# One kernel for six sublayers: ScalarE's order written out in two stages, weights quantized in pieces, transposes of a pair ahead of their copies

## The chip, the core and the metric

The kernel runs on one NeuronCore of a Trainium2 chip. A core has engines with queues of their own: TensorE (PE, matrix products and transposes, into PSUM), VectorE (DVE), ScalarE (ACT), GpSimd (POOL) and SyncE (SP, which here only starts transfers). They meet at semaphores. An engine works through its own queue in order. The metric is the device time of one execution in microseconds, lower is better; the median of several runs stands for a kernel. One more execution was profiled, and what the profile says is of that one.

## What is computed

The input `x` is 8 sequences of 1024 tokens with 256 numbers each, 8192 tokens in float32. Six sublayers follow, each on a layer norm of `x` and added to `x`:

```python
x = x + 0.5 * _L0_ffn_ref(_layernorm(x), w_gate, w_up, w_down)        # fp4
x = x + _L0_attn_ref(_layernorm(x), Wqkv_w, Wqkv_b, out_w, out_b, gamma_raw)   # decay
x = x + 0.5 * _L0_ffn_ref(_layernorm(x), w_gate, w_up, w_down)        # fp4 again
x = x + 0.5 * _L1_ffn_ref(_layernorm(x), W1, b1, W2, b2)              # ternary
x = x + _L1_attn_ref(_layernorm(x), w_q, w_k, w_v, w_o, gate, memories, memory_norms)
x = x + 0.5 * _L1_ffn_ref(_layernorm(x), W1, b1, W2, b2)              # ternary again
```

The fp4 feed-forward quantizes every operand in blocks of 16 numbers: a scale (largest magnitude / 6), rounding to the grid 0, 0.5, 1, 1.5, 2, 3, 4, 6, and the scale again. It computes `silu(x Wg) * (x Wu)`, quantizes that too, and multiplies by `Wd` (704 hidden numbers). The weights are quantized inside the kernel. The ternary feed-forward divides each weight matrix by its mean magnitude, rounds to -1, 0 or 1, and uses a GELU between (1024 hidden numbers).

The decay attention is a linear attention with one decay `sigmoid(gamma_raw)` per head. The memory attention, 16 heads of 16, is this:

```python
sq = elu1(q); sk = elu1(k)                     # elu + 1
out_m = einsum('bhsd,mhde->mbhse', sq, memories) / clip(einsum('bhsd,mhd->mbhs', sq, memory_norms))
weights = softmax(mean over s of the divisors)
mem_out = sum over m of weights * out_m
num = einsum(sq, cumsum(sk x v));  den = einsum(sq, cumsum(sk))
out = sigmoid(gate) * mem_out + (1 - sigmoid(gate)) * num / den,  then  out @ w_o.T
```

## The kernel before

All of `x` stays in SBUF, 16 tiles `X[g]` of 4 x 128 tokens. A group is 512 tokens, a unit 128 of them: 16 groups, 64 units. The six stages run one after the other, called at the end of `macaron_kernel`: `ffn_fp4(True, "decay")`, `attn_decay("fp4")`, `ffn_fp4(False, "ternary")`, `ffn_ternary(False, "memory")`, `attn_memory("ternary")`, `ffn_ternary(True)`. Only the first prepares weights beside its units (`prepare`).

**Order.** An instruction given to `pin` (lines 172 to 188) follows the last pinned one of its engine: the order is written by hand. What is not pinned is placed by the framework's scheduler, which may draw it forward to where its inputs are ready. Before the change TensorE and VectorE are pinned nearly everywhere; ScalarE is pinned nowhere in the fp4 stages and the memory attention. `behind` (line 190) makes a block of preparation start behind the last pinned instructions.

**Statistics.** `statistics(sizes, dues)` (line 232) splits the layer norm's statistics of all groups into small shares for VectorE (`bn_stats`, `bn_aggr`, then a seed and four Newton steps), handed out by `advance(u)` one unit at a time. `PLANS` says how many groups are taken together and when they are due. The first set of a stage is computed by `begin` during the last units of the stage before. `normalize` (line 273) is two ScalarE instructions for each of a group's four tiles.

**The start** (lines 388 to 461). The raw weights and the first tile come in by DMA on the queues of SP, ScalarE and GpSimd. `scale_part` and `round_part` quantize the halves of the gate and up weights and the first `xn`: maxima and rounding on VectorE, magnitudes (`Abs` with a factor) on ScalarE, both multiplications on GpSimd; TensorE turns the weights.

**An fp4 stage** (`ffn_fp4`, line 602). For unit `i` of group `g` (`j` = `i` mod 4), `hidden(i)` makes for two halves `q` the products `pg` and `pu` (line 685), `sg = silu(pg)` on ScalarE (694) and `h = sg * pu` on VectorE (695). `scale` (632) and `round_` (650) quantize `h`; `q_sc` is a small ScalarE copy, `qp` holds magnitudes. `turn(i-2)` transposes `h` into two PSUM tiles `pt` which ScalarE copies to `ht`; `down(i-3)` multiplies by `wd` into `po` (727), and VectorE adds it to `x` (736). The next group's `xn` is normalized at `j` = 0, scaled at 1, rounded at 2; at `j` = 3, between `pg` and `pu` of the second half, `norm_turn` transposes it (`transpose_group`, line 350): four transposes, a copy (361), four transposes, a copy. The pool of `pt` has two buffers, shared by `xt` and `ht`.

Beside the units of the first stage (`first`, line 741): at 0 and 1 `prep_down`, at 1 the turning of the down weights and `load_a0`, at 5 `prep_decay` (the decays' exponentials and tables), at 6 and 9 the loads of `w1`, `w2`, at 8 and 11 `prep_ternary` in one piece (sum on VectorE, total `pa` by a matmul in the bank of `po`, two halves rounded on VectorE), at 12 `prep_memory`.

**The memory attention** (`attn_memory`, line 1202) is a pipeline: in step `i` the keys and values of unit `i`, the scores of unit `a` = `i-1`, the weighted sum of `b` = `i-2`, the division of `c` = `i-3`, and outputs of `d`, `e`. `keys(i)` (1369) makes the products `pkv` and three ScalarE results: `vz` (1387), `kd` (1394, not in the last unit of a sequence) and `qz` (1398), two masked copies of the queries `sq`, which need nothing of `keys` itself. The scores `sc` (917) of the next step need `qz`. TensorE's order in a step: memory products `pmo` (1410) among scores `sc`, `py`, `psd`, in the last step of a group the divisors `pr`, then the transposes `pyt` of `y` and `pn` of `nt` (in that last step of a group both in one PSUM tile, `pyn`), a projection `pk` or `pq` of a group two ahead (1015), the output `po`, and `keys(i)`. VectorE makes `at` (926), `mo` (1423), `rw` (1549), `y`, and the sum into `x` (1619). ScalarE further makes `nt`, `state`, `yt`, `ee` (1255) and `xt`. Groups 0 to 2 are projected in an opening before the steps; units 56 to 63 have no projection left to do.

Of the kernel before, what the change touches and what calls it, by code (L numbers as in the profile page):

```python
# [17 lines left out]
P = 128  # L18
# [20 lines left out]
def macaron_kernel(  # L39
# [52 lines left out]
    w_f0 = f0_stack.enter_context(tc.tile_pool(name="w_f0", bufs=1))  # L92
    raw_stack = ExitStack()
# [34 lines left out]
    gsig = w_l1.tile([P, H], F32, name="gsig")  # L128
    nc.sync.dma_start(out=gsig, in_=gate.partition_broadcast(P))
# [102 lines left out]
    def statistics(sizes, dues):  # L232
# [40 lines left out]
        def normalize(dst, g, only=None):  # L273
            for j in range(G) if only is None else (only,):
                n = G * g + j
                nc.scalar.activation(
                    dst[:, j, :], X[g][:, j, :], AF.Identity, bias=lb[:, n : n + 1]
                )
                nc.scalar.activation(dst[:, j, :], dst[:, j, :], AF.Copy, scale=lr[:, n : n + 1])
# [16 lines left out]
            (GB + 1, 2, 3, 4, NG), [max(0, G * (g - GB) - 3) for g in range(NG)]  # L296
# [95 lines left out]
    with (  # L392
# [6 lines left out]

        def scale_part(v, bank, at):  # L400
# [15 lines left out]
            def round_part():  # L416
                mg = prep_q.tile([P, nb * 16], F32, tag="q_mg", name="q_mg")[:np_]
# [30 lines left out]
        round_g()  # L448
        weights_turn(wg_n, wg, 0)
        round_u()  # L450
# [3 lines left out]
        round_x()  # L454
# [7 lines left out]

    def prep_down(c):
        fp4_round(wd_n[:, c, :], fp4_scale(wd_n[:, c, :], raw, nc.vector, pin), raw, nc.gpsimd, pin)
# [11 lines left out]
    a0_stack = ExitStack()  # L476
    A0 = SimpleNamespace()

    def load_a0():
        w_a0 = a0_stack.enter_context(tc.tile_pool(name="w_a0", bufs=1, side="right"))  # L480
# [6 lines left out]
        A0.lng = w_a0.tile([P, H + 2], F32, name="lng")  # L487
        A0.dec = w_a0.tile([P, 4, 4, P], F32, name="dec")
        A0.gq = w_a0.tile([P, 2, P], F32, name="gq")
        A0.gk = w_a0.tile([P, H], F32, name="gk")  # L490
        A0.gs = w_a0.tile([P, 2], F32, name="gs")
# [5 lines left out]
        nc.sync.dma_start(out=A0.lng[:, 0:H], in_=gamma.partition_broadcast(P))  # L497
        nc.sync.dma_start(out=A0.lng[:, H : H + 2], in_=gamma_rep.rearrange("(m p) -> p m", p=P))

    def prep_decay(prep):  # L500
# [4 lines left out]

        ea = prep.tile([P, H + 2], F32, tag="ea", name="ea")
        nc.scalar.activation(ea, A0.lng, AF.Abs)
# [94 lines left out]
    def ffn_fp4(prepare, after):  # L602
        with ExitStack() as st:
# [94 lines left out]
            def rounding(i):  # L698

                parts = []  # L700
                if i % G == 2 and i // G + 1 < NG:
                    parts.append(x_part(i // G + 1))
# [980 lines left out]
```

## Time and profile before

| | us |
|---|---|
| median of 3 runs (2856.53 to 2856.86) | 2856.61 |
| profiled execution | 2854.04 |
| its span, first to last instruction | 2851.3 |

The stages, from the profile's windows (busy us of each engine; edges read from the timeline to some us):

| stage | window, us | length | PE | DVE | ACT | POOL |
|---|---|---|---|---|---|---|
| start | 0 to 45 | 45 | 9.8 | 34.5 | 16.5 | 24.2 |
| fp4, first | 45 to 650 | 605 | 540.2 | 464.1 | 270.4 | 251.1 |
| decay attention | 650 to 1115 | 465 | 459.1 | 304.7 | 187.1 | 4.5 |
| fp4, second | 1115 to 1675 | 560 | 528.6 | 429.8 | 246.9 | 235.0 |
| ternary, first | 1675 to 1940 | 265 | 262.3 | 181.4 | 166.5 | 0.2 |
| memory attention | 1940 to 2584 | 644 | 582.5 | 498.7 | 317.8 | 299.1 |
| ternary, second | 2584 to 2851 | 267 | 262.4 | 176.1 | 162.5 | 0.0 |

How to read it: where an engine's busy time is near the length of its window, that engine sets the stage's time. Lines of the profile give, for a group of instructions, its source line, engine, operation, output and inputs by name, and the idle time in front of it with what released it: `PE pt L712 <- ACT xt L361` is TensorE waiting, at its instruction of line 712, for ScalarE's instruction of line 361. A busy TensorE is not one at its peak.

Unit lengths, by the starts of `po` at line 727: 7.98 us in a plain unit, 9.05 in a `j` = 3 unit without a wait for `xt`, 10.84 with one. In the memory attention, twelve groups (2038.28 to 2491.70, by `pyn`) take 453.4 us, 37.8 each.

### The profile page before, as it was taken

The page shows a single profiled execution, that of the slowest core. Times are in us where ns is not written, and L with a number is a line of the kernel's source. Part 1 is how long each engine was busy: PE and PEld are TensorE (multiplying, and loading weights), DVE is VectorE, ACT ScalarE, POOL GpSimd, SP SyncE. Part 2 cuts the span into 40 slices and gives each one's busy share as a digit, 9 for nine tenths or more (in the row PEclk, how much of TensorE's full clock was granted, in tenths as well). Part 3 has the DMA queues.
Part 4 walks back from the last instruction along what each step waited for, and adds up shares of the span by engine and source line. Part 5 has one row for each costly group of instructions (what it writes and reads, how often), then busy time and mean ns, then how long its engine had stood idle before and what let it go on. Part 6 is the DMA issues. An engine that isn't in the chain of part 4 may idle for free.

```text
span 2851.3 us, 53491 instructions
## 1 busy us (share of the span) xinstructions
PE 2644.8 (93%) x21536; PEld 1996.1 (70%) x21536; DVE 2089.3 (73%) x4732; ACT 1367.7 (48%) x3000; POOL 814.1 (29%) x760
## 2 busy tenths in 40 slices
PE   3779999999999998999999999998999999988999
PEld 2557777776676666677776779995666666667998
DVE  7787878776666667887878778555788877877654
ACT  3534444444434333444444456565455555435665
POOL 4434444430000002444444410001455455531000
PEclk9889999999999999999999999999999999999999
DMA  5100000000000000000000000000000000000011
GB/s 166 32 17 1 1 1 1 1 1 1 2 2 2 2 2 1 1 1 1 1 1 1 1 1 1 1 1 1 2 2 2 2 2 2 2 2 16 30 38 38
DMA packets 26228, 27.04 MB, mean 9 GB/s; under 512 B 5116, under 2 KB 25084, under 8 KB 25980
## 3 DMA queue, kind: packets, MB, share of 16 engines
q1 hardware_dynamic: 24838, 21.66, 2.4%
q8 instruction: 169, 2.77, 0.4%
q10 hardware_dynamic: 998, 1.44, 0.2%
q14 instruction: 79, 0.65, 0.1%
q0 software_dynamic: 144, 0.52, 0.1%
HBM read 15.23 MB, written 8.39 MB: 8 GB/s over the span
## 4 chain that ended last, share of the span: by engine, by line
PE 72%; DVE 16%; POOL 4%; ACT 4%; issue 2%; DMA 0%; POOLq 0%; DVEq 0%; ACTq 0%
PE po L874 9%; PE po L727 8%; PE ph L848 8%; PE pg L685 7%; PE pu L685 7%; PE py L1001 4%; PE sc L917 4%; PE po L1015 4%; PE pk L1015 4%; PE pkv L1015 3%; PE pq L1015 3%; DVE h L656 3%; PE py L983 2%; DVE qp L636 2%; DVE xn L656 1%
## 5 line engine op out<-in xcount | busy, mean ns | idle before, releaser
L727 PE MATMUL po<-wd,ht 128*128 128x256 f32 (+1 forms) x1536 | 359.9, 384 | 7.0 <-DVE x L736 6.5
L685 PE MATMUL pu<-wu,xt 128*128 128x352 f32 x1024 | 348.9, 463 | 11.0 <-DVE h L695 10.8
L685 PE MATMUL pg<-wg,xt 128*128 128x352 f32 x1024 | 348.5, 462 | 6.5 <-ACT sg L694 6.0
L727 PEld LDWEIGHTS po<-wd,ht 128*128 128x128 f32 (+1 forms) x1536 | 285.7, 193 | 45.1 <-DVE x L736 8.3
L660 POOL TENSOR_TENSOR h<-h,q_sc 128x704 f32<-128x704 f32 x128 | 177.5, 1387 | 451.9 <-DVE h L656 451.9
L685 PEld LDWEIGHTS pu<-wu,xt 128*128 128x128 f32 x1024 | 193.3, 192 | 114.5 <-DVE h L695 11.9
L695 DVE TENSOR_TENSOR h<-sg,pu 128x352 f32<-128x352 f32 x256 | 129.7, 516 | 187.4 <-PE pu L685 179.8
L685 PEld LDWEIGHTS pg<-wg,xt 128*128 128x128 f32 x1024 | 194.6, 191 | 100.2 <-ACT sg L694 10.9
L874 PE MATMUL po<-w,hl 128*128 128x256 f32 x1024 | 250.5, 282 | 1.1 <-DVE hl L859 1.1
L874 PE MATMUL po<-w,hh 128*128 128x256 f32 x1024 | 249.8, 282 | 0.0
L1582 POOL TENSOR_TENSOR y<-y,mo 128x256 f32<-128x256 f32 x256 | 210.2, 821 | 131.6 <-DVE y L1575 117.9
L656 DVE SCALAR_TENSOR_TENSOR h<-qp,h 128x704 f32<-128x704 f32 x256 | 227.2, 888 | 18.4 <-ACT qp L653 13.9
L859 DVE TENSOR_TENSOR hl<-hf,hh 128x512 fp32r<-128x512 f32 x256 | 168.0, 686 | 64.7 <-ACT hh L857 60.4
L848 PE MATMUL ph<-xh,w 128*128 128x512 f32 x512 | 203.6, 399 | 0.9 <-DVE x L1619 0.5
L694 ACT ACTIVATE sg<-pg 128x352 f32<-128x352 f32 x256 | 118.2, 462 | 177.7 <-PE pg L685 177.7
L848 PE MATMUL ph<-xl,w 128*128 128x512 f32 x512 | 200.6, 393 | 0.0
L644 POOL TENSOR_TENSOR h<-h,q_rs 128x704 f32<-128x704 f32 x128 | 177.6, 1387 | 71.4 <-DVE q_rs L640 54.2
L874 PEld LDWEIGHTS po<-w,hl 128*128 128x128 f32 x1024 | 195.0, 190 | 2.4 <-DVE hl L859 1.7
L874 PEld LDWEIGHTS po<-w,hh 128*128 128x128 f32 x1024 | 194.3, 190 | 1.8
L926 DVE TENSOR_TENSOR at<-sc,tri 128x512 f32<-128x512 f32 x256 | 171.4, 670 | 20.3 <-PE py L1001 17.2
L856 ACT ACTIVATE hf<-ph,b1c 128x512 f32<-128x512 f32 x256 | 167.7, 701 | 17.5 <-PE ph L848 17.4
L926 DVE TENSOR_TENSOR at<-sc,dec 128x512 f32<-128x512 f32 x256 | 158.5, 681 | 18.9 <-PE sc L917 18.9
(257 smaller groups left out, 5576.6 us busy)
## 6 DMA issues: line engine op xcount, KB each, us to landing
x<-in_x SPq DMA_DIRECT2D x15, 512.0 KB, 8.9
out<-x SPq DMA_DIRECT2D x15, 512.0 KB, 2.9
raw_w<-in_w_t SPq DMA_DIRECT2D x2, 1024.0 KB
wqkv<-in_wqkv_t SPq DMA_DIRECT2D x1, 768.0 KB
wu_n<-in_w_up ACTq DMA_DIRECT2D x2, 352.0 KB
wg_n<-in_w_gate SPq DMA_DIRECT2D x2, 352.0 KB
wd_n<-in_w_down ACTq DMA_DIRECT2D x1, 704.0 KB, 14.4
x<-in_x POOLq DMA_DIRECT2D x1, 512.0 KB, 10.9
```

The source lines that it names most:

```text
L644: nc.gpsimd.tensor_tensor(vb, vb, rs[:, :, None].to_broadcast([P, nb, 16]), ALU.mult)
L656: nc.vector.scalar_tensor_tensor(v, mg, FP4_LEAST, v, ALU.max, op)
L660: nc.gpsimd.tensor_tensor(vb, vb, sc[:, :, None].to_broadcast(list(vb.shape)), ALU.mult)
L685: nc.tensor.matmul(ps, lhsT=xt[:, k, j * P : (j + 1) * P], rhs=w[:, k, cols], start=(k == 0), stop=(k == 1),)
L727: nc.tensor.matmul(po, lhsT=ht[:kn, c, :], rhs=wd[:kn, c, :], start=(c == 0), stop=(c == len(DCH) - 1),)
L848: nc.tensor.matmul(ph, lhsT=w1[:, k, f * P : (f + 1) * P], rhs=xt[:, k, :], start=(k == 0 and xt is xh), stop=(k == 1 and xt is xl),)
L856: nc.scalar.activation(hf, ph, AF.Gelu, bias=b1c[:, f : f + 1])
L859: nc.vector.tensor_tensor(hl[:, f, :], hf, hh[:, f, :].bitcast(F32), ALU.subtract)
L874: nc.tensor.matmul(po, lhsT=ht[:, f, j * P : (j + 1) * P], rhs=w2[:, f, :], start=False, stop=(f == NF - 1 and ht is hl),)
L926: nc.vector.tensor_tensor(at, sc.rearrange("p m (e t) -> p (m e) t", e=2), weight, ALU.mult)
L1015: nc.tensor.matmul(dst, lhsT=lhsT, rhs=rhs, start=n == 0, stop=n == len(parts) - 1)
L1582: nc.gpsimd.tensor_tensor(yv, yv, mo_c[:, :, :, m, :].rearrange("p r c n -> p c r n"), ALU.add)
```

## The change

- `gamma` and `gate` are loaded at the start, on ScalarE's queue ahead of `wu_n` and `wd_n`; the decays' pool is opened there. The Sigmoid of `gsig`, `ea`, the index tables and the exponentials `dec`, `gq`, `gk`, `gs` move from `prep_decay` and `prep_memory` into the start phase, pinned; `prep_decay` keeps the multiplications by `tri`.
- The start's magnitudes of three operands go to a PSUM tile `mg0`.
- `prep_down` is split: scaling (multiplication now on GpSimd) at units 0 and 1, rounding at 1 and 2, turning at 2.
- `prep_ternary` returns four pinned pieces, run one a unit at 8 to 11 (`w1`, loaded at 6) and 15 to 18 (`w2`, loaded at 13); `prep_memory` moves from 12 to 20.
- In the fp4 stages ScalarE is pinned: `sg`, the `q_sc` copies, the magnitudes, the second `sg`, `xt`, the normalization, `ht`. At `j` = 3 both halves of `xn` are transposed first (`turn_products`); the two copies stand behind the second `sg`.
- In the memory attention ScalarE is pinned in the order of the program. At each step both transposes `pyt` and `pn` come ahead of the copy `yt`. In the last eight units `keys` goes to bank 2 and comes ahead of the output product. `advance` moves behind the sum into `x`. The memory plan takes five groups first instead of three.

The core of the diff:

```diff
+    A0.lng = w_a0.tile([P, H + 2], F32, name="lng")
+    nc.scalar.dma_start(out=A0.lng[:, 0:H], in_=gamma.partition_broadcast(P))
+    nc.scalar.dma_start(out=A0.lng[:, H : H + 2], in_=gamma_rep.rearrange("(m p) -> p m", p=P))
+    gsig = w_l1.tile([P, H], F32, name="gsig")
+    nc.scalar.dma_start(out=gsig, in_=gate.partition_broadcast(P))
...
-            (GB + 1, 2, 3, 4, NG), [max(0, G * (g - GB) - 3) for g in range(NG)]
+            (GB + 3, 3, 4, NG), [max(0, G * (g - GB) - 3) for g in range(NG)]
...
+        mg0 = prep_pq.tile([P, 1024], F32, name="mg0")
...
+        pin(nc.scalar.activation(gsig, gsig, AF.Sigmoid))
...
+        def decays():
...
+            for h in range(H):
+                pin(
+                    nc.scalar.activation(
+                        A0.dec[:, h % HT // 2, h // HT * 2 + h % 2, :], df, AF.Exp,
+                        scale=A0.lng[:, h : h + 1],
+                    )
+                )
...
         ln.normalize(xn, 0)
         begun["fp4"] = (ln, xn)
-        round_g()
+        decays()
+        round_g(mg0)
...
+    def prep_down_scale(c):
+        wd_sc[c] = fp4_scale(wd_n[:, c, :], raw, nc.gpsimd, pin)
+
     def prep_down(c):
-        fp4_round(wd_n[:, c, :], fp4_scale(wd_n[:, c, :], raw, nc.vector, pin), raw, nc.gpsimd, pin)
+        fp4_round(wd_n[:, c, :], wd_sc.pop(c), raw, nc.gpsimd, pin)
...
+        return sums, total, lambda: rounded(0), lambda: rounded(1)
...
+            def prepared(i):
+
+                if 1 <= i < 3:
+                    prep_down(i - 1)
+                if i < 2:
+                    prep_down_scale(i)
+                if i == 2:
+                    prep_down_turn(ps_t, "pt")
...
+                for k, i0 in enumerate((6, 13)):
...
+                    if i0 + 2 <= i < i0 + 6:
+                        raw_w[1][i - i0 - 2]()
...
+            for i in range(NT + 3):
                 g, j = divmod(i, G)
+                ahead = g + 1 < NG
+                h = hp.tile([P, NI], F32, tag="h", name="h") if i < NT else None
                 if i == 0:
-                    norm_turn(0)
-                if i < NG * G:
-                    hidden(i)
+                    xts[0], copied = turn_products(xts[0])
+                    copied()
+                for q in range(2):
+                    if i < NT:
+                        pg = ps_h.tile([P, NHALF], F32, tag="pg", name="pg", bufs=1)
+                        pu = ps_h.tile([P, NHALF], F32, tag="pu", name="pu")
+                        products(i, q, wg, pg)
+                        if q == 1 and j == 3 and ahead:
+
+                            xts[g + 1], copied = turn_products(xts[g + 1][0])
+                        products(i, q, wu, pu)
+                        gated(h, q, pg, pu)
+                    if q == 0:
+                        while copies:
+                            copies.pop(0)()
+                    elif i < NT and j == 3 and ahead:
+                        copied()
+
+                    if 0 < i <= NT and q == (1 if j == 3 else 0):
+                        magnitudes(hs[i - 1][0], qp[:, 0:NI])
...
+                if i < NT and j == 0 and ahead:
+                    norm(g + 1)
+                if 0 <= i - 2 < NT:
+                    turn(i - 2)
...
+                if 0 <= i - 3 < NT:
+                    down(i - 3)
                 if prepare:
...
+                    prepared(i)
...
-            def keys(i):
+            def keys(i, at):
...
-                pkv = bank(3, [P, 2, D], "pkv")
+                pkv = bank(at, [P, 2, D], "pkv")
...
-                nc.scalar.copy(
-                    vz[:, :, 0::2, :],
-                    pkv[:, 1, :].rearrange("p (r e i) -> p r e i", e=2, i=HD),
+                pin(
+                    nc.scalar.copy(
+                        vz[:, :, 0::2, :],
+                        pkv[:, 1, :].rearrange("p (r e i) -> p r e i", e=2, i=HD),
+                    )
                 )
...
-                    nc.scalar.copy(kd, pkv[:, 0, :])
+                    pin(nc.scalar.copy(kd, pkv[:, 0, :]))
...
                 for e in range(2):
-                    nc.scalar.activation(
-                        qz[:, :, e, :], sq[:, :, cols], AF.Copy, scale=pm[:, e : e + 1]
+                    pin(
+                        nc.scalar.activation(
+                            qz[:, :, e, :], sq[:, :, cols], AF.Copy, scale=pm[:, e : e + 1]
+                        )
                     )
...
-                    yt = cp.tile([P, 2, P], F32, tag="yt", name="yt")
-                    nc.scalar.copy(yt, pyt)
-                    ys[d] = yt
                 if 0 <= c < n:
                     nt, mo_c, rw_c = chunk.pop(c)
                     for m in range(2):
                         pin(nc.tensor.transpose(pn[:, m, :], nt[:, m, :], ident))
+                if 0 <= d < n:
+                    yt = cp.tile([P, 2, P], F32, tag="yt", name="yt")
+                    pin(nc.scalar.copy(yt, pyt))
+                    ys[d] = yt
...
-                if 0 <= e < n:
+                def output():
...
+                if elu and 0 <= e < n:
+                    po = output()
...
                 if i < n:
-                    keys(i)
+                    keys(i, 3 if elu else 2)
                 if elu:
                     elu()
+                elif 0 <= e < n:
+                    po = output()
```

## The prediction

> **What bounds the kernel now.** I read the page's busy times and its chain first, then the waits of TensorE stage by stage, then timelines of ScalarE and TensorE around the waits that the change touches.
>
> The busy times and the chain:
>
> ```profile
> PE 2644.8 (93%) x21536; PEld 1996.1 (70%) x21536; DVE 2089.3 (73%) x4732; ACT 1367.7 (48%) x3000; POOL 814.1 (29%) x760
> PE 72%; DVE 16%; POOL 4%; ACT 4%; issue 2%; DMA 0%; POOLq 0%; DVEq 0%; ACTq 0%
> ```
>
> TensorE is busy 2644.8 of 2851.3 us. No arithmetic leaves it, so the change can only work on the 206 us in which it idles. ScalarE, whose order is rewritten, is busy 48%: it can cost only where TensorE waits for one result of it. So I list TensorE's waits: the first fp4 stage, steady part (200 to 640 us), its beginning (45 to 200), and the memory attention (1990 to 2580). Columns: total us, times, longest.
>
> ```profile
> PE pt L712 <- ACT xt L361: 16.5, 10, 1.8
> ```
> ```profile
> PE pa L550 <- DVE t_ab L546: 17.8, 2, 10.4
> PE ptd L470 <- POOL wd_n L348: 9.1, 1, 9.1
> PE pg L685 <- ACT sg L694: 5.2, 3, 4.4
> ```
> ```profile
> PE pyn L1572 <- ACT yt L1567: 12.7, 13, 1.0
> PE py L983 <- DVE mo L1423: 11.2, 16, 1.5
> PE sc L917 <- DVE at L926: 6.7, 7, 1.7
> PE po L1015 <- DVE rw L1549: 4.8, 8, 0.7
> PE pmo L1410 <- DVE lg L1328: 4.6, 4, 3.1
> ```
>
> In the steady fp4 stage one wait is nearly everything; 1120 to 1670, the second fp4 stage, has the same line with 19.6 us in 12, so 36.1 together. In the memory attention the waits are many and small. What is *not* there matters most: no score waits for its queries `qz`. Around 2199 us (TensorE) and 2207 us (ScalarE):
>
> ```profile
> 2198.83 0.38 PE L1015 MATMUL pkv<-wkv,xt 128*128 128x256 f32 x1
> 2199.16 0.50 PE L917 MATMUL sc<-qz,sk 32*128 32x256 f32 x3
> ```
> ```profile
> 2200.75 0.91 ACT L1398 ACTIVATE qz<-sq,pm 128x256 f32<-128x256 f32 x2 [1.13 <-PE pmo L1410]
> 2207.60 0.37 ACT L1387 COPY vz<-pkv 128x256 f32<-128x256 f32 x1 [1.20 <-PE pkv L1015]
> 2207.87 0.38 ACT L1394 COPY kd<-pkv 128x256 f32<-128x256 f32 x1
> ```
>
> The scores start as the key and value products end (2199.16 against 2198.83 + 0.38). The two `qz` writes run at another time, after scores have released a buffer: ScalarE makes them one or two units early.
>
> **The change part by part.** The sums are made in the profiled execution's time, 2854.04 us with a span of 2851.3; the median of the runs, 2856.61, is 2.6 above it, which I add at the end.
>
> *fp4 stages.* A group's four transposes of `xn` go twice into the two PSUM buffers, and TensorE's next transposes (of `h`) wait there for the second copy on ScalarE:
>
> ```profile
> 394.36 0.63 PE L712 MATMUL pt<-ident,h 128*128 128x128 f32 x4 [1.79 <-ACT xt L361]
> ```
>
> In the change both halves are transposed first and ScalarE copies them right behind the second `sg`, under the matmuls of `pu` (4 x 0.38 us). The 36.1 us go. What is late next: a `down` of 2.76 us (twelve matmuls at 395.04) needs the VectorE addition of the one before. When a statistics tile (0.57 us) stands ahead of that addition, I expect about half of it as a wait once a group: 30 x 0.29 = 8.6. The eight normalisation instructions (eight at 0.5 = 4.0 us) now stand in one piece on ScalarE ahead of the `ht` copies; these have a unit's time (7.98 us between two `down`s) until their `down`, which hides the 4.0; uncovered they would cost up to 1 us a group. Sum: -36.1 + 8.6 = **-28**, bounds -36 (no new wait) and -6 (1 us in each of 30 groups).
>
> *The first units.* Between the third and the eleventh `down` (104.92 and 203.95) pass 99.0 us; eight units at the steady pace of 33.0 a group take 66, so 33 go to preparing weights. On ScalarE in that stretch:
>
> ```profile
> 104.33 1.28 ACT L508 ACT_TABLE_LOAD   x1
> 115.39 4.76 ACT L519 ACTIVATE dec<-df,lng 128x128 f32<-128x128 f32 x16
> 120.95 1.28 ACT L694 ACT_TABLE_LOAD   x1
> 122.24 0.47 ACT L694 ACTIVATE sg<-pg 128x352 f32<-128x352 f32 x1
> ```
>
> `sg` at 122.24 stands behind a table, 16 `dec`, three small ones and another table; TensorE waits 4.4 us and its next `pg` takes 2.72 instead of 1.35, `pu` 2.47. Moving these ahead of the units saves 4.4 + 1.4 + 1.1, about 7. The ternary weights are now summed in one unit, totalled in the next and rounded in two more. The total's matmul `pa` writes the bank of `po`; its 17.8 us of waits shrink to the wait for an addition of `x` and the total behind it, by a walk over the VectorE rows 5 and 3: saves 10. Against it: each rounding piece is 1.2 + 2 x 0.7 = 2.6 us on VectorE inside a unit; I charge half, four times, 5; and 16 multiplies of `dec` by `tri` (7.2 us on GpSimd) still run in one go before the scaling of `h`, 2. Sum: -7 - 10 + 5 + 2 = **-10**, bounds -20 (no charge, `pa` quick) and +5 (the roundings and the multiplies in full).
>
> How TensorE runs after a wait matters for all of this: after 4.4 us of idleness `pg` took double, after the 1.79 us above the transposes took 0.63, as the others do; so I charge the waits of 1.5 us below with themselves alone.
>
> On the table loads a rule and the rows differ. The rows show 1.28 us for a load and the activation 0.01 to 0.02 behind it, so four loads fewer are 5.1 us of ScalarE. The Trainium skill, "ScalarE: Activation LUTs", section What ACT_TABLE_LOAD costs, counts a drain of 1.38 us with each switch, some 2.66 in all: by it four loads are 10.6 us, and the first units' sum would be nearer -15 than -10. The rows decide.
>
> *The start.* ScalarE's queue gets three more DMA issues ahead of `wd_n`'s (about 0.47 each) and 16 + 4 exponentials (4.76 + 1.2). TensorE is there busy 18.3 of 55 us, so most hides behind the loads and GpSimd's scaling. The down weights' scaling moves from VectorE to GpSimd, and TensorE already waits 9.1 us for their last GpSimd step: no gain there. **+1**, bounds -3 and +6 (all exponentials in the way).
>
> *Memory attention: what is added.* With ScalarE written out, the order in a unit is `vz`, `kd`, then the two `qz` of the same unit, and the scores that need them are TensorE's next work. On ScalarE: start 0.04 behind the products, 0.27 until `kd` can start, 0.27 until `qz`, 0.91: 1.5 us. Bounds: 1.7 with no overlap (0.04 + 0.37 + 0.38 + 0.91), 1.25 if the first memory products run meanwhile. TensorE's in-order work behind it is the whole unit. Units 1 to 55 pay: 55 x 1.5 = +82, less 2 for seven units without `kd`. In the last eight units, keys now come before the output product (1.03), which leaves 0.5: +4.
>
> *What is removed.* `pyn` behind `yt`: -12.7, since both transposes now precede the copy. The last units' wait for `rw`: -4.8, as the output product moves back. The opening: TensorE stands 5.4 us at 1973.7 behind statistics and the next products take 3.78 for 1.88 and 1.64 for 1.03; the new plan does five groups of statistics in the ternary stage, where VectorE has room: -7.9, less 2.5 for normalisation now behind an exponential. A VectorE that is late catches up in 1.5 us a unit: `at` and `lg` go (-11.3), of `mo` half (-5.6). Sum: 80 + 4 - 12.7 - 4.8 - 5.4 - 16.9 = **+44**. Bounds: at 1.25 with all of `mo` gone, 69 + 4 - 12.7 - 4.8 - 7.9 - 22.5 = +25, or +15 if VectorE's lateness hides in durations too; at 1.7 with nothing caught up, 92 + 4 - 12.7 - 4.8 - 5.4 = +73.
>
> *Total.* -28 - 10 + 1 + 44 = **+7**: 2861 profiled, **2864** as a median. Two nearly equal sums oppose each other, so the sign is weakly held.
>
> **The rivals.**
>
> *The wait is swallowed and the kernel is faster.* In the memory attention VectorE was what ended last in many units (`mo`, `at`, `lg`, 22.5 us of shown waits, more inside score durations: the scores of 2216.67 took 1.87). If 0.7 us of the wait only replaces these in each unit, 55 x 0.7 = 38 are caught up instead of 16.9, and memory costs +22; with fp4 at -34, the first units at -16 and the start at 0 the sum is -28: 2829. It decides from about 0.7 us of VectorE's lateness in a unit. For it: VectorE has 467 of 590 us of work there. Against: in 1990 to 2580 TensorE's whole idleness was 51 us, and 82 cannot fit into it.
>
> *The normalisation block takes the fp4 gain.* Eight instructions of ScalarE in one piece hold up `ht` and the next `sg`. At 1 us a group the fp4 stages give only -6; with the rest as above the sum is +29: 2886. It decides once ScalarE's backlog at the end of the first unit of a group is over the 4 us that lie between the block and the next unit's first `sg`. For it: 4.4 us behind `dec` reached TensorE at once. Against: there ScalarE was held 8.3 us, not 4.
>
> *The scores do not wait.* If `qz` is ready anyway, memory keeps only what is removed (-12.7 - 4.8 - 5.4), -23, and the sum is -60: 2797. Little speaks for it: `qz` of a unit stands behind its `kd` in ScalarE's order, and nothing else writes it.
>
> **How the numbers follow.** 0.2% is 5.7 us, about what can be told from no change. Forecast 0.46 (0.40 of it slower by more, 0.06 within); normalisation block 0.14, slower; swallowed wait 0.34 (0.32 faster, 0.02 within); no wait 0.06, faster. So slower 0.54, same 0.08, faster 0.38. The forecast's own range is 2850 to 2885. For 8 in 10 the range runs from 2815, the faster rival with some 14 us of the bounds, to 2900, the slower one with as much; outside lie no wait (0.06) and the corners where several bounds meet.
>
> **What would show it.** Right: `PE pt <- ACT xt` gone in both fp4 stages and their groups at 33 to 33.6 us; a new line `PE sc <- ACT qz` with 55 waits of about 1.5; memory groups from 37.8 to about 41 us; `pyn <- yt` gone; eight table loads instead of twelve. Wrong: the new line under 0.8 us each (first rival), a line `pg <- ACT sg` or `po <- ACT ht` in the fp4 stages (second), or scores that still follow the products at once (third). A change in the decay attention or the ternary stages of over 3 us would be something that I have not seen.

## The result and the profile after

| | before | after |
|---|---|---|
| median, us | 2856.74 (4 runs, 2856.53 to 2858.43) | 2873.47 (4 runs, 2872.49 to 2878.55) |
| ratio | 1 | 1.0061, 95% interval 1.0043 to 1.0078 |
| profiled execution | 2854.04 | 2872.56 |
| its span | 2851.3 | 2870.9 |

The change makes the kernel slower by 0.6%, by 16.7 us between medians and 19.6 us between spans. Behind this small sum stand large terms of both signs. I compared the starts of the same TensorE instructions in both profiled executions; a stretch that became shorter is negative:

| stretch | before, us | after, us | difference |
|---|---|---|---|
| to the first `down` | 89.0 | 102.9 | +14.0 |
| from there to `down` of unit 20 | 201.4 | 194.1 | -7.3 |
| units 20 to 62, first fp4 stage | 354.5 | 339.0 | -15.5 |
| end of fp4 and decay attention, to the next fp4 stage's first `down` | 493.6 | 492.1 | -1.5 |
| units 0 to 62, second fp4 stage | 528.4 | 508.7 | -19.7 |
| from there to the last `ph` of the first ternary stage | 255.8 | 256.3 | +0.5 |
| from there to the first `ph` of the second ternary stage: memory attention | 661.8 | 709.2 | +47.4 |
| rest | 263.7 | 265.5 | +1.8 |

The page of the changed kernel, busy times and chain:

```profile
PE 2671.9 (93%) x21536; PEld 2018.8 (70%) x21536; DVE 2087.3 (73%) x4715; ACT 1369.2 (48%) x2996; POOL 816.1 (28%) x762
PE 78%; DVE 10%; ACT 6%; POOL 3%; issue 2%; DMA 0%; ACTq 0%; POOLq 0%; DVEq 0%
```

No engine has more instructions to do, and ScalarE's busy time hardly moves (1367.7 to 1369.2). TensorE's rises by 27.1 us for the same 21536 instructions, 22 of them in the memory attention; below, part of a wait is seen to be filled there and so to count as busy. In the chain of work that ended last, VectorE's share fell from 16% to 10% and ScalarE's rose from 4% to 6%. TensorE's waits after the change, in the steady part of the first fp4 stage:

```profile
PE pt L744 <- POOL h L692: 3.3, 2, 2.6
PE pa L589 <- DVE x L768: 2.7, 1, 2.7
```

`pt <- xt`, 16.5 us before, is gone. In its beginning (45 to 200 us):

```profile
PE ptd L539 <- POOL wd_n L360: 10.6, 2, 7.8
PE pg L721 <- ACT sg L732: 9.1, 2, 7.0
PE pa L589 <- DVE x L768: 5.1, 1, 5.1
```

`pa` fell from 17.8 to 5.1 in this window (another 2.7 comes later), but `pg` waits 7.0 us for one `sg`. In the memory attention (1930 to 2600):

```profile
PE sc L980 <- ACT qz L1464: 49.1, 56, 1.5
PE py L1046 <- DVE mo L1490: 12.6, 12, 2.1
```

The new line at the top is the predicted one. Only 0.9 us is shown in most of its 56 waits; the whole delay is read from a unit. Its two timelines, TensorE and ScalarE:

```profile
2220.31 1.03 PE L1078 MATMUL pkv<-wkv,xt 128*128 128x256 f32 x4
2221.27 0.71 PE L1477 MATMUL pmo<-memb,sq 32*128 32x128 f32 x4
2222.88 1.17 PE L980 MATMUL sc<-qz,sk 32*128 32x256 f32 x16 [0.90 <-ACT qz L1464]
```
```profile
2221.37 0.37 ACT L1451 COPY vz<-pkv 128x256 f32<-128x256 f32 x1 [0.69 <-PE pkv L1078]
2221.64 0.38 ACT L1459 COPY kd<-pkv 128x256 f32<-128x256 f32 x1
2221.91 0.92 ACT L1464 ACTIVATE qz<-sq,pm 128x256 f32<-128x256 f32 x2
```

The products end at 2221.34, `vz` starts at 2221.37, `qz` is done at 2222.83 and the scores start at 2222.88: 1.54 us. That is also the median of the 64 units; in the kernel before it is -0.06, no wait at all. A first set of `pmo`, which the scores would otherwise have run among, fills part of it, so the line of waits counts 0.9.

### The profile page after: what moved, and what is told of

Its sections match the earlier page's. It is cut to its first block, busy times and chain, and to the rows that moved or that the text cites. A ratio compares the mean times of both kernels' runs of the same rounds, so it can differ in the third digit from the quotient of the medians.

```text
span 2870.9 us, 53376 instructions
## 1 busy us (share of the span) xinstructions
PE 2671.9 (93%) x21536; PEld 2018.8 (70%) x21536; DVE 2087.3 (73%) x4715; ACT 1369.2 (48%) x2996; POOL 816.1 (28%) x762
## 3 DMA queue, kind: packets, MB, share of 16 engines
q10 hardware_dynamic: 1558, 1.46, 0.2%
## 4 chain that ended last, share of the span: by engine, by line
PE 78%; DVE 10%; ACT 6%; POOL 3%; issue 2%; DMA 0%; ACTq 0%; POOLq 0%; DVEq 0%
PE po L759 10%; PE pg L721 9%; PE pu L721 9%; PE po L937 8%; PE ph L911 8%; PE py L1064 4%; PE sc L980 4%; PE po L1078 4%; PE pk L1078 4%; PE pkv L1078 4%; PE pq L1078 3%; PE py L1046 2%; PE pt L744 2%; DVE h L689 1%; ACT qz L1464 1%
## 5 line engine op out<-in xcount | busy, mean ns | idle before, releaser
L721 PE MATMUL pg<-wg,xt 128*128 128x352 f32 x1024 | 354.3, 469 | 14.1 <-ACT sg L732 13.8
L759 PEld LDWEIGHTS po<-wd,ht 128*128 128x128 f32 (+1 forms) x1536 | 283.9, 191 | 46.0 <-DVE x L768 10.4
L919 ACT ACTIVATE hf<-ph,b1c 128x512 f32<-128x512 f32 x256 | 168.9, 703 | 17.8 <-PE ph L911 17.7
```

What stands on the lines that cost most here:

```text
L721: nc.tensor.matmul(ps, lhsT=xts[g][:, k, j * P : (j + 1) * P], rhs=w[:, k, q * NHALF : (q + 1) * NHALF], start=(k == 0), stop=(k == 1),)
L759: nc.tensor.matmul(po, lhsT=ht[:kn, c, :], rhs=wd[:kn, c, :], start=(c == 0), stop=(c == len(DCH) - 1),)
L919: nc.scalar.activation(hf, ph, AF.Gelu, bias=b1c[:, f : f + 1])
```

## The experiments

My theory had three parts: the memory attention loses to `qz` behind `kd`; the fp4 stages gain because the copies of `xt` stand behind both halves; and the beginning loses to what was moved into it. The rivals said that VectorE sets the pace in the memory attention, that ScalarE's written order as such made the gain, and that other work in the beginning takes the place of what is removed. The diffs are cut to their core.

### qz_ahead: the changed kernel, the two qz in front of vz

```diff
             def keys(i, at):
...
+                qz = cp.tile([P, 2, 2, P], F32, tag="qz", name="qz")
+                for e in range(2):
+                    pin(
+                        nc.scalar.activation(
+                            qz[:, :, e, :], sq[:, :, cols], AF.Copy, scale=pm[:, e : e + 1]
+                        )
+                    )
                 pkv = bank(at, [P, 2, D], "pkv")
...
-                qz = cp.tile([P, 2, 2, P], F32, tag="qz", name="qz")
...
                 chunk[i] = (vz, kd, qz)
```

> The changed kernel with one thing moved: in keys the two qz writes stand ahead of vz and kd in ScalarE's written order, so they run under the pkv products. Theory (the memory attention loses to qz standing behind kd): the line sc <- qz, 49.1 us in 56, goes; VectorE's lateness comes back for some 10; memory groups fall from 40.9 to about 37, the time by 35 to 49 from 2873, to 2825 to 2840. Rival (VectorE sets the memory attention's pace and the wait only stands in front of it): the wait turns into waits for mo and at, groups stay over 39.5, the time at 2855 or more.

Measured: 2826.07 us (before on the same chip 2857.82; ratio 0.9889, interval 0.9874 to 0.9904), 47 us below the changed kernel. ScalarE of this kernel, around one unit:

```profile
2231.20 0.92 ACT L1439 ACTIVATE qz<-sq,pm 128x256 f32<-128x256 f32 x2
2232.22 0.37 ACT L1458 COPY vz<-pkv 128x256 f32<-128x256 f32 x1
```

`qz` runs while TensorE makes `pkv` (2231.16 to 2232.19), when ScalarE has nothing else. The memory attention takes 661.6 us, 47.6 less. The theory holds: the place of two instructions of 0.46 us in ScalarE's order was the whole net loss of this stage. But 661.6 is also what the kernel before took (661.8), although the wait for `yt` is gone. In its place stands this (1990 to 2580):

```profile
PE py L1046 <- DVE mo L1489: 33.5, 34, 2.2
```

The line had 11.2 us before and 10.9 after the change. So the rival has a part: once TensorE no longer waits for ScalarE, VectorE ends last.

### before_qz_behind: the kernel before, vz, kd and qz pinned in this order

```diff
-                nc.scalar.copy(
-                    vz[:, :, 0::2, :],
...
+                pin(
+                    nc.scalar.copy(
+                        vz[:, :, 0::2, :],
...
-                    nc.scalar.copy(kd, pkv[:, 0, :])
+                    pin(nc.scalar.copy(kd, pkv[:, 0, :]))
...
-                    nc.scalar.activation(
-                        qz[:, :, e, :], sq[:, :, cols], AF.Copy, scale=pm[:, e : e + 1]
+                    pin(
+                        nc.scalar.activation(
+                            qz[:, :, e, :], sq[:, :, cols], AF.Copy, scale=pm[:, e : e + 1]
+                        )
```

> The kernel before with vz, kd and qz of a unit pinned in this order on ScalarE, nothing else. Theory: this part alone costs about what the memory attention lost: 1.5 us in 55 units less caught-up lateness, groups from 37.8 to 41 or 42, the time from 2857 to 2895 to 2915. Rival (the loss comes from the rest of the pinned order, such as the eight normalization instructions in one piece or the moved copy of yt): under 15 us, below 2872.

Measured: 2924.67 (1.0234, 1.0218 to 1.0249), 67 us slower than before, 10 above the expected range. This part alone costs more than the whole change loses; most groups take 41.3 to 43.0 us, a few 44.5 to 47.2. So the rest of the change in this stage had gained: 731.1 us here against 709.2 in the changed kernel.

### yt_between: the changed kernel, the copy yt between pyt and pn

```diff
                         pin(nc.tensor.transpose(pyt[:, m, :], y[:, m, :], ident))
+                    yt = cp.tile([P, 2, P], F32, tag="yt", name="yt")
+                    pin(nc.scalar.copy(yt, pyt))
+                    ys[d] = yt
...
                         pin(nc.tensor.transpose(pn[:, m, :], nt[:, m, :], ident))
-                if 0 <= d < n:
-                    yt = cp.tile([P, 2, P], F32, tag="yt", name="yt")
-                    pin(nc.scalar.copy(yt, pyt))
-                    ys[d] = yt
```

> The changed kernel with the copy yt of the memory attention back between the transposes pyt and pn. Theory (the shared transposes ahead of the copy save 1.0 us in 13 groups, and qz's wait had left TensorE alone in setting the pace): the line pyn <- yt is back with about 12.7, the time rises by 9 to 13, to 2882 to 2887. Rival (VectorE or GpSimd, late with y and mo, takes what is saved there): within 4 of 2873.5.

Measured: 2889.71 (1.0117, 1.0102 to 1.0132), 16 us above the changed kernel; `pyn <- yt` is back with 12.6 in 13, and groups are 42.0 instead of 40.9. Transposes ahead of their copy are worth this much in a stage where TensorE sets the pace. Of the 21.9 us between the stage in `before_qz_behind` and in the changed kernel this explains 16.7 (here the stage took 725.9).

### q_advance: qz_ahead, the statistics back in front of the projection

```diff
                 if "sum" in held:
                     running_sum(*held.pop("sum"))
+                if i < n:
+                    ln.advance(i)
...
                     pin(nc.vector.tensor_tensor(xe, po, xe, ALU.add))
-                if i < n:
-                    ln.advance(i)
```

> The kernel qz_ahead (2826.1) with ln.advance of the memory attention back in front of the projection, as before the change. Theory (its 34 waits py <- mo of 33.5 us come from the pieces of statistics, 0.57 us each, that now stand in VectorE's order between the sum into x and mo): the line falls to 12 or less, groups from 37.5 to 36 to 37, the time by 10 to 25, to 2801 to 2816. Rival (VectorE is short of time there and the wait only moves, to at and to rw): within 6 of 2826.

Measured: 2828.64 (0.9899, 0.9882 to 0.9916), 2.6 above `qz_ahead`: the theory falls. From 1930 to 2580 us `py <- mo` did fall, from 34.7 to 22.3, but `sc <- at` rose from 0.8 to 4.7 and `pmo <- lg` appeared with 3.6, and the groups stayed at 37.0 to 40.7. The wait moved.

### copy_between: the changed kernel, each copy of xt behind its own transposes

```diff
                     pts.append(pt)
-
-                def copied():
-                    for k, pt in enumerate(pts):
-                        pin(nc.scalar.copy(xt[:, k, :], pt))
-
-                return xt, copied
+                    pin(nc.scalar.copy(xt[:, k, :], pt))
+
+                return xt, lambda: None
```

> The changed kernel, but in the fp4 stages each copy to xt stands right behind its own four transposes in ScalarE's order, ahead of the second sg; all else stays pinned. Theory (the gain of the fp4 stages comes from the copies standing behind both halves): a wait at pt for the copy, or at pg for an sg that is late, is back, 1 to 2 us in most of 30 groups, the time rises by 20 to 50, to 2893 to 2923. Rival (ScalarE's written order as such made the gain): within 8 us of 2873.

Measured: 2876.08 (1.0064, 1.0049 to 1.0079), 2.6 above the changed kernel with overlapping runs (2871.84 to 2880.01 against 2872.49 to 2878.55); the stretches of the fp4 stages are the same to 0.2 us. My theory fell. The order of these copies against their transposes and `sg` is worth nothing here. What is? In the kernel before, ScalarE at a `j` = 3 unit:

```profile
391.04 0.47 ACT L694 ACTIVATE sg<-pg 128x352 f32<-128x352 f32 x1
392.94 0.76 ACT L653 ACTIVATE qp<-h 128x704 f32<-128x704 f32 x1 [1.43 <-POOL h L644]
393.63 1.06 ACT L361 COPY xt<-pt 128x512 f32<-128x512 f32 x2
```

The transposes were done at 391.4. The copies stand behind the magnitudes `qp` of `h`, which waited 1.43 us for GpSimd. Both changed kernels have the magnitudes last:

```profile
392.83 1.08 ACT L709 COPY xt<-pt 128x512 f32<-128x512 f32 x2
393.78 0.50 ACT L728 ACTIVATE sg<-pg 128x352 f32<-128x352 f32 x1
394.73 0.76 ACT L685 ACTIVATE qp<-h 128x704 f32<-128x704 f32 x1 [0.45 <-POOL h L678]
```

(This is `copy_between`.) From this came the next run.

### before_xt_first: the kernel before, only the copies of xt and the magnitudes pinned

```diff
-            if k == 0 or both_act:
+            if tag == "pt":
+                pin(nc.scalar.copy(dst[:, k, :], pt))
+            elif k == 0 or both_act:
                 nc.scalar.copy(dst[:, k, :], pt)
...
                 for v, sc, mg in parts:
-                    nc.scalar.activation(mg, v, AF.Abs, scale=FP4_MAGIC)
+                    pin(nc.scalar.activation(mg, v, AF.Abs, scale=FP4_MAGIC))
```

> The kernel before with only the two copies to xt and the magnitudes of the fp4 stages pinned on ScalarE in the order of the program: at j = 3 the copies come ahead of the magnitudes of h, which wait for GpSimd. Theory (in the kernel before, the scheduler put those magnitudes in front of the copies; 1.43 us of waiting and 0.76 of work stood before them, and this is the whole of the 1.79 us wait): the line pt <- xt goes from both fp4 stages, the time falls by 30 to 37, to 2820 to 2827. Rival (it takes the rest of the written order too, sg and ht, or the transposes of both halves): less than half of it, over 2840.

Measured: 2820.64 (0.9872, 0.9856 to 0.9889). Three changed lines make the kernel faster by 36 us. In the two fp4 stretches of the table above they gain 12.9 and 18.2 us of the 15.5 and 19.7 that the whole change gained; the remaining 4 are not in these lines. The steady part of its first fp4 stage (200 to 640 us) has a 3.3 at `pt <- POOL h`, 1.3 at `po <- x`, and no `pt <- xt`. This settles the cause of the wait: the copies of `xt` had been behind an instruction that waited for GpSimd.

### loads_sp: the changed kernel, gamma and gate on SP's queue

```diff
-    nc.scalar.dma_start(out=A0.lng[:, 0:H], in_=gamma.partition_broadcast(P))
-    nc.scalar.dma_start(out=A0.lng[:, H : H + 2], in_=gamma_rep.rearrange("(m p) -> p m", p=P))
...
-    nc.scalar.dma_start(out=gsig, in_=gate.partition_broadcast(P))
...
         nc.scalar.dma_start(out=wu_n[:, part, :], in_=wu_v[:, part, :])
+    nc.sync.dma_start(out=A0.lng[:, 0:H], in_=gamma.partition_broadcast(P))
+    nc.sync.dma_start(out=A0.lng[:, H : H + 2], in_=gamma_rep.rearrange("(m p) -> p m", p=P))
+    nc.sync.dma_start(out=gsig, in_=gate.partition_broadcast(P))
```

> The changed kernel with the loads of gamma and gate on SP's queue behind the gate weights, so that ScalarE's queue begins with wu_n again. Theory (the three small loads hold back wu_n, whose first reduction began at 15.0 instead of 8.95 us): wu_n's reduction starts near 9 us, the first pg near 38 instead of 43.7, the time falls by 4 to 7, to about 2867. Rival (the exponentials and three table loads on ScalarE in the start hold everything): the first pg stays within 2 us of 43.7, the time within 2.

Measured: 2878.32 (1.0071, 1.0054 to 1.0088), 5 slower than the changed kernel, where I expected faster. Half of the theory held: the first reduction of `wu_n` starts at 8.94 instead of 15.00 us. But then the first pinned instruction of ScalarE waits for a load that is late itself:

```profile
15.82 0.21 ACT L419 ACTIVATE gsig<-gsig 128x16 f32<-128x16 f32 x1 [5.85 <-DMA gsig<-in_gate]
29.36 1.01 ACT L481 ACTIVATE mg<-wg_n 88x1024 f32<-88x1024 f32 x1
```

In the changed kernel the two stood at 11.11 and 14.49, in the kernel before the magnitudes of `wg_n` ran at 11.07. So both matter: small loads ahead of `wu_n` delay it, and tables and exponentials ahead of the magnitudes delay those. (The start's magnitudes are not pinned: in the changed kernel the scheduler placed those of `wg_n` ahead of the exponentials, here behind them.) The first `pg` is at 49.3.

### q_start, q_down, q_ternary: qz_ahead with one part of the preparation as before

`q_start` takes back the start (loads, Sigmoid, exponentials, `mg0`), `q_down` the split of the down weights, `q_ternary` the four units of each ternary weight:

```diff
-        decays()
-        round_g(mg0)
+        round_g()
```
```diff
-    wd_sc[c] = fp4_scale(wd_n[:, c, :], raw, nc.gpsimd, pin)
+    wd_sc[c] = fp4_scale(wd_n[:, c, :], raw, nc.vector, pin)
...
-                if 1 <= i < 3:
-                    prep_down(i - 1)
                 if i < 2:
                     prep_down_scale(i)
-                if i == 2:
+                    prep_down(i)
+                if i == 1:
```
```diff
-                    if i0 + 2 <= i < i0 + 6:
-                        raw_w[1][i - i0 - 2]()
+                    if i == i0 + 2:
+                        for piece in raw_w[1]:
+                            piece()
```

> qz_ahead with the start as before the change: gamma and gate on SP's queue late, Sigmoid and the decays' exponentials back in the preparation beside the units (not pinned), no mg0. Theory (the moved loads and exponentials cost 6 us in the start and save about 7 at unit 3): the first pg at 38 instead of 43.7, four more table loads and a wait pg <- sg of about 4 us between units 2 and 4; within 6 of 2826. Rival (the start's delay is paid in full, and the exponentials beside the units cost little now that ScalarE is pinned): 6 to 12 faster, 2814 to 2820.

Measured: 2823.10 (0.9879, 0.9865 to 0.9894), 3 below `qz_ahead`. The first `pg` comes at 37.4 instead of 43.4 and the first `down` 9.0 earlier; at unit 20 only 2.8 of this is left, and at the first `down` of the second fp4 stage nothing (0.1). As the theory has it, what moving the exponentials saves beside the units is about what it costs in the start. The 3 us of the median appear later, in the second fp4 stage (505.5 us instead of 508.7), which the edit does not touch; why is not shown.

> qz_ahead with the down weights scaled on VectorE, rounded at units 0 and 1 and turned at unit 1, as before the change. Theory (the split made the first down later: 59.2 us after the first pg instead of 51.4): first down 5 to 9 us earlier against the first pg, the time 4 to 9 lower, 2817 to 2822. Rival (the first units are bound by rounding work on VectorE and GpSimd, and the first down only trades places with it): within 3 of 2826.

Measured: 2820.97 (0.9873, 0.9858 to 0.9887), 5 below `qz_ahead`. The first `down` stands 54.4 us behind the first `pg`, against 60.8, and at the `down` of unit 62 in the second fp4 stage the kernel is 7.3 ahead: the theory holds. (Some 4 us of it are lost in the memory attention's end, for a reason that has nothing to do with the edit; it is told below.)

> qz_ahead with all four pieces of each ternary weight in one unit (8 and 15) instead of four. Theory (pieces save 10 us of waits at pa): the wait at pa <- t_ab is back, 7 to 10 us for each weight, the time 8 to 16 higher, 2834 to 2842. Rival (TensorE pays the same VectorE work either way, in pieces it pays it as waits for x, h and sg): within 4 of 2826.

Measured: 2824.91 (0.9884, 0.9870 to 0.9899), 1 below `qz_ahead`, where the theory had 8 to 16 above. In one piece `pa` waits 10.3 us in two from 45 to 260 us, in pieces 7.8 in two; the pieces pay more than that elsewhere: from the first `down` to that of unit 20 the kernel in one piece takes 188.4 us and `qz_ahead` 194.2. At the `down` of unit 62 in the second fp4 stage it is 4.3 ahead (it too loses this in the memory attention's end). By the median the rival holds; by the profile quantizing in pieces even costs 4 to 6 us.

### best and two_orders

`best` joins `qz_ahead`, the parts of `q_start` and `q_down`, and the normalization of group 1 moved from unit 0 to unit 1 (it had held back `sg` by 7.0 us):

```diff
-                if i < NT and j == 0 and ahead:
+                if ahead and i == (1 if g == 0 and prepare else G * g):
                     norm(g + 1)
```

> All the undoings that gained, together: qz ahead of vz, the start and the exponentials as before the change, the down weights as before, and the normalization of group 1 at unit 1 instead of unit 0, since its eight instructions held back sg there for 7.0 us. Theory (they act in different stretches, so they add: 2826.1 less 3, 5 and 3 to 7): 2809 to 2815, and the wait pg <- sg of 7.0 at the beginning gone. Rival (the first units are bound by preparation on VectorE and GpSimd, and each gain there is taken by the next wait): 2817 or more.

Measured: 2819.56 (0.9869, 0.9855 to 0.9884): 6.5 below `qz_ahead`, the rival's number, but not for the rival's reason. The first `down` comes at 90.7 instead of 104.2, and of these 13.5 us 10.6 are left at unit 20 and 10.7 at the `down` of unit 62 in the second fp4 stage. Four are lost in the last 98 us of the memory attention, whose code and waits are the same in both: this stretch (from the last `pyn` to the next stage's first `ph`) takes 94.1 us in `qz_ahead` and 98.0 in `best`. Its windows, `qz_ahead` and then `best` (TensorE's busy time is the third number, its granted clock the third from the end):

```profile
2462.00:2556.00 94.00, 70.18 (x1057) 54.28 (x1054) 63.72 (x154) 28.53 (x86) 38.97 (x56) 0.97 0.01 2
```
```profile
2451.40:2549.40 98.00, 75.44 (x1056) 57.62 (x1055) 63.73 (x154) 28.54 (x86) 38.95 (x56) 0.90 0.01 2
```

The same thousand matrix instructions take 5.3 us longer at a clock of 0.90 instead of 0.97. So the gains of `q_start` and `q_down` do add (2.8 and 7.3 at unit 20, of the 10.6), and about 0.5 is left for the move of the normalization, expected at 3 to 7; a lower clock later took part of the sum. Within the first units `pg <- sg` keeps 10.4 us from 45 to 260, the longest 5.2, so the wait of 7.0 is shorter, not gone.

`two_orders` is `before_xt_first` with the transposes `pyt` and `pn` ahead of the copy `yt`, nothing else:

```diff
-                    yt = cp.tile([P, 2, P], F32, tag="yt", name="yt")
-                    nc.scalar.copy(yt, pyt)
-                    ys[d] = yt
...
                         pin(nc.tensor.transpose(pn[:, m, :], nt[:, m, :], ident))
+                if 0 <= d < n:
+                    yt = cp.tile([P, 2, P], F32, tag="yt", name="yt")
+                    nc.scalar.copy(yt, pyt)
+                    ys[d] = yt
+                if 0 <= c < n:
```

> before_xt_first (2820.6) with the transposes pyt and pn of the memory attention ahead of the copy yt, ScalarE otherwise not pinned there. Theory (VectorE is late in this stage as soon as TensorE is not held: what pyn saves comes back at py <- mo and sc <- at): pyn <- yt gone, mo and at up by most of it, the time within 5 of 2820.6. Rival (the 12.7 us are free, as the run yt_between showed on the changed kernel): 2806 to 2812.

Measured: 2815.69 (0.9852, 0.9836 to 0.9869), 5 below `before_xt_first` and the fastest kernel here, 41.9 below the kernel before of the same runs. Its largest wait in the memory attention (1990 to 2580):

```profile
PE py L985 <- DVE mo L1425: 18.2, 25, 1.5
```

`pyn <- yt`, 12.7 us, is gone; `py <- mo` rose from 10.3 to 18.2 and `po <- rw` from 4.8 to 6.0. VectorE takes back most of it, as the theory said. Even the 5 us are not certain: the stage took 661.5 us here, 665.5 in `before_xt_first` and 661.8 in the kernel before, and these two have the same code in it, at a mean granted clock of 0.97 and 0.98. Against the kernel before, at the same clock of 0.98, the edit is worth 0.3 us. The same edit gained 16 us in the changed kernel, where TensorE waited for `qz` in every unit and VectorE could catch up.

## Why the prediction was right, and where it was not

Forecast was 2864 in a range of 2815 to 2900, slower; it is 2873.5. The sum is nearer than its terms, and that is luck: the fp4 stages gave some 11 us more than forecast, the start cost 13 more and the first units gave 6 less. By terms:

- **Memory attention, +44 predicted, +47.4 measured.** Place, cause and size were right. 1.5 us a unit is 1.54 in the trace, groups "about 41" are mostly 40.86 (41.2 in the mean), `pyn <- yt` is gone. Of the smaller terms, half of `mo` did not go: its line is 10.9 us after 11.2 (1990 to 2580). That VectorE catches up behind the wait is seen from the other side: without the wait, in `qz_ahead`, `py <- mo` is three times as large. What the prediction listed as removed (`yt`, `rw`, the opening) is therefore real only beside the wait: `qz_ahead` has them removed and its stage is as long as that of the kernel before, so with the wait taken out the other edits gained nothing net.
- **fp4 stages, -28 predicted, -38.8 measured:** -35.2 in the two stretches of the table, and 3.6 for two waits for `xt` between 200 and 290 us, ahead of unit 20, which the 36.1 include. The line went, as said, and the charge of 8.6 for later additions of `x` was mis-sized: `po <- x` is 2.1 and 3.6 in the two stages, against 0.7 and 3.2 before. The cause was wrong in the step that had the 36.1 us go because both halves are transposed first and copied behind `sg`: `copy_between` undoes that and loses nothing. What counts is that the copies stand ahead of the magnitudes, which wait for GpSimd; `before_xt_first` shows it alone. The row that says so, 1.43 us of ScalarE's idleness ahead of `qp`, was in the profile of before; I read the wait's releaser and did not look at what stood in front of the releaser.
- **First units, -10 predicted, -3.7 measured:** -7.3 up to unit 20, less the 3.6 of `xt` that belong above. The exponentials were sized well: beside the units they cost 6.1 us in `q_start`, 7 were predicted, and the table loads are eight instead of twelve. The pieces of the ternary weights had the wrong sign: -10 for `pa` and +5 for the roundings were forecast; `pa` did fall, but `q_ternary` is 5.8 us shorter in this stretch without the pieces.
- **The start, +1 predicted with bounds of -3 and +6, measured +14.0 to the first `down`.** This is the mis-sized term. Of it 6.2 lie before the first `pg`. I had counted the three issues on ScalarE's queue (0.47 each) and not their transfers, nor that the pinned Sigmoid waits for them: `wu_n` is reduced at 15.00 instead of 8.95, and VectorE starts to round the gate weights at 22.50 instead of 17.19. The exponentials come on top: VectorE then waits 4.45 us for the magnitudes of `wu_n`, which ScalarE makes at 28.35, behind the last `dec`, though GpSimd was done with `wu_n` at 19.74. Part of this is made up again, as rounding `wu_n` takes 2.47 us instead of 4.08; why is not shown.

The other 7.8 of the start lie between the first `pg` and the first `down`. Most of it is the split of the down weights, for which the prediction charged nothing: without it `q_down` has 6.3 less here. The wait of 7.0 for `sg` cannot simply be added, because it stands in the place of one of the kernel before (45 to 200 us):

```profile
PE pu L685 <- DVE h L695: 7.8, 1, 7.8
```

Nor is it the work of group 1's eight normalizations, which the prediction priced at 4.0 and hidden. They are pinned ahead of this `sg` (66.02), and the first of them waits for VectorE's statistics itself:

```profile
60.44 0.51 ACT L283 ACTIVATE xn<-x,ln_b 128x256 f32<-128x256 f32 x1 [4.77 <-DVE ln_b L228]
```

**The rivals.** VectorE did not swallow the wait for `qz`, but it swallowed what was gained elsewhere in that stage once `qz` was out of the way. The normalization block did hold up `sg`, for 7.0 us, behind unit 0 only; in the steady parts the line `pg <- sg` is 1.5 us in all (200 to 640) and absent (1130 to 1650). The scores did wait.

What stays open: whether the transposes ahead of `yt` gain anything in the kernel before; which instruction of VectorE's order would have to move for `mo` to be in time once TensorE is not held (`q_advance` tried one and only moved the wait), and whether the pinned order of `best` and the three lines of `before_xt_first` could be joined into something faster than `two_orders`; this was not tried.

## What to carry to other kernels

Writing an engine's order by hand moves every instruction, and one of them can cost more than the rest gains: look, for each instruction that another engine waits for, at what stands directly in front of it and at what that waits for (the copies of `xt` stood behind magnitudes that waited for GpSimd, the `sg` of 66.02 behind a normalization that waited for VectorE). An instruction that only needs old data belongs ahead of the ones that wait, as `qz` ahead of `vz`. And a wait that is removed is worth its time only where no other engine is just behind: the same reordering was worth 16 us under a wait and at most 5 without it.

## What the runs showed of the hardware

Three small loads at the head of ScalarE's queue (18 and 16 numbers on each of 128 partitions; the queue's packets rise from 998 to 1558) were expected to cost their issue, 1.4 us in all. The load behind them, issued at 2.27 instead of 0.81 us, was used 6.0 us later than before, at 15.00, and the last small one itself, issued at 1.72, at 11.11. With the three on SP's queue behind the gate weights, `wu_n` was used at 8.94 again and the small one at 15.82.

TensorE's clock also fell behind waits shorter than the prediction reckoned with. It charged waits of 1.5 us with themselves alone, and for the waits of `qz` this held (most groups take 40.85 to 40.87). In the end of the memory attention, though, two waits near each other, 2.15 us for `mo` and 1.81 for `y`, were followed in `best` by a mean granted clock of 0.68 to 0.83 for some 12 us; the next `po` took 1.91 us instead of 1.03. After the same two waits, 2.14 and 1.80, `qz_ahead` ran on at full clock. The kernels differ there only in when the waits come. Taken in windows of 3.4 us, `best` shows a clock of 0.50 from 2458.14 to 2461.55 and from 2464.97 to 2468.38, and 1.00 in the windows between and around; in the windows ahead of these two TensorE was busy 1.27 and 1.61 us. In `qz_ahead`, in windows from 2464.46 on, the waits fall on other places of the windows; the least busy have 1.95 and 1.74 us, and the clock stays at 1.00. These rows fit a clock that follows how busy the window before was, but no run varied this, and a limit does not come out of them. Not all of the 4 us between the two kernels come from this place: 2.8 are lost there, and in the last 16 us of the stage `best` has a clock of 0.61 and `qz_ahead`, in its last 14.5, one of 0.90. Differences of 4 us between kernels of this family are therefore not read from their medians alone.
